# A recommender's user stage: some history rows fetched one by one from SyncE

## The chip, the core and the metric

The kernel runs on one core of a Trainium2 chip. A core has TensorE (PE), which multiplies matrices, VectorE (DVE) and ScalarE (ACT), which work on rows, GpSimd (POOL), which issues the gathers here, SyncE (SP), which issues plain transfers, and 16 DMA engines that carry out what is issued. The metric is device time in microseconds (us), lower is better. Each kernel is run several times; the number given is the median.

## What is computed

For 16384 users there are 100 history items each and one target item, out of 50001 items. Each item has an embedding of 64 values and two attention results of 32 values each over its 32 neighbours. The reference, cut to what matters:

```python
near_full = concat([near_pois, pad_row])
a_sus = _neighbor_attn(E_in, near_full)          # per item: softmax(E . E[near]) over 32 neighbours
a_inf = _neighbor_attn(E_out, near_full)
h = concat([E_hist[history], a_sus[history], a_inf[history]], -1)   # B x 100 x 128
t = concat([E_tgt[target], a_inf[target], a_sus[target]], -1)       # B x 128
x = h * t[:, None, :]
z = relu(einsum('bld,hd->blh', x, W1) + b1)
scores = einsum('blh,h->bl', z, W2[0])
exp_A = exp(scores) * ((history != target[:, None]) & (history != 0))
attn = exp_A / (sum(exp_A, -1) ** 0.5)[:, None]
s = sum(h * attn[..., None])                      # one number
pred = sigmoid(cosine(broadcast s, t))            # B
```

## The kernel before, in words

The work has two stages, and the second needs all of the first.

The item stage makes two tables in device memory. `table` holds one row of 128 floats (512 bytes) per item for use as history, `ttab` one per item for use as target. It goes through the items in 23 blocks; POOL gathers the neighbours' rows with one indirect transfer per neighbour (L111, `v`), VectorE and ScalarE do the attention, and SyncE writes the finished rows out (L163 `table`, L164 `ttab`). SyncE also loads each block's inputs (L102, L104, L106).

The user stage works on 128 users at a time, one to a partition. There are 128 such columns `c`. The 100 history places of a column are cut into 25 groups `g` of four. For a group, POOL issues four indirect transfers (L233): each fetches one history row for each of the 128 users into the tile `h`. PE turns the four blocks round (L246, `hT_ps`), VectorE multiplies them by the turned target row `tT` (L248, `xT`) and sums the plain rows (L249, `hsum`), PE applies W1 (L255, `z_ps`), ScalarE the relu (L257, `z`), and PE the vector W2, one column of `score` for each of the four places (L265). At the end of a column ScalarE and VectorE make the weights and two sums (L271 on).

The loop over `s` puts the groups of all columns in one row and works on three at once: `gather` and `turn` of group s, `hidden` of s-1, `scored` of s-2. Twelve `h` tiles let POOL run ahead by up to twelve groups. The target rows of the next column are gathered half way through a column (L197, `t`). The history numbers are loaded for four columns at a time, by SyncE (L193, `hidx`, 128 x 400 integers, two buffers); SyncE has nothing else to do in this stage until the result is written (L325). Each engine runs its own instructions in order; semaphores, which the framework sets, hold a reader until its writer is done. A transfer also waits for the one issued eight before it from the same kind of queue, since eight semaphores are used in turn.

Of the kernel before, what the change touches and what calls it, by code (L numbers as in the profile page):

```python
# [9 lines left out]

F32 = mybir.dt.float32
I32 = mybir.dt.int32
AF = mybir.ActivationFunctionType
ALU = mybir.AluOpType
AX = mybir.AxisListType

P = 128
ITEMS = 50001
# [3 lines left out]
D = 128  # L22
HID = 128
B = 16384
L = 100
# [10 lines left out]
UC = B // P  # L36
BSUB = 4
LG = 4
NG = L // LG


@with_exitstack
def kernel(
# [13 lines left out]
    nc = tc.nc  # L57
# [5 lines left out]
    table = dram.tile([ROWS, D], F32, name="table")  # L63
# [29 lines left out]
    with (  # L93
# [6 lines left out]
        for it in range(NITER):  # L100
            nidx = n_in.tile([P, NSUB, K], I32, name="nidx")
            nc.sync.dma_start(nidx, near_v[it])  # L102
# [5 lines left out]
            for j in range(NSUB):  # L108
                v = n_v.tile([P, K, 2, G], F32, name="v")
                for k in range(K):  # L110
                    nc.gpsimd.indirect_dma_start(  # L111
                        out=v[:, k].rearrange("p t d -> p (t d)"),
# [20 lines left out]
                for t in range(2):  # L133
                    nc.scalar.activation(  # L134
                        ex[:, t, :],
                        sc[:, t, :],
                        AF.Exp,
                        bias=top[:, t : t + 1],
# [32 lines left out]
    hist_v = history.rearrange("(p i j) l -> i p j l", p=P, j=BSUB)  # L171
    tidx = const.tile([P, UC], I32, name="tidx")
    nc.scalar.dma_start(tidx, target.rearrange("(p c) -> p c", p=P))
    tidf = const.tile([P, UC], F32, name="tidf")
    nc.vector.tensor_copy(tidf, tidx)
    with (
        tc.tile_pool(name="u_in", bufs=2) as u_in,
        tc.tile_pool(name="u_t", bufs=2) as u_t,
        tc.tile_pool(name="u_h", bufs=12) as u_h,
        tc.tile_pool(name="u_x", bufs=3) as u_x,  # L180
        tc.tile_pool(name="u_s", bufs=2) as u_s,
        tc.tile_pool(name="ps_t", bufs=3, space=bass.MemoryType.PSUM) as ps_t,
        tc.tile_pool(name="ps_z", bufs=3, space=bass.MemoryType.PSUM) as ps_z,
        tc.tile_pool(name="ps_s", bufs=2, space=bass.MemoryType.PSUM) as ps_s,
    ):
        users = {}
        hists = {}

        def target_rows(c):

            if c % BSUB == 0:
                hidx = u_in.tile([P, BSUB, L], I32, name="hidx")
                nc.sync.dma_start(hidx, hist_v[c // BSUB])  # L193
                hists[c // BSUB] = hidx

            t = u_t.tile([P, D], F32, name="t")
            nc.gpsimd.indirect_dma_start(  # L197
                out=t,
                out_offset=None,
                in_=ttab[0:ITEMS, :],  # L200
                in_offset=bass.IndirectOffsetOnAxis(ap=tidx[:, c : c + 1], axis=0),
            )
            users[c] = {"t": t, "hidx": hists[c // BSUB][:, c % BSUB, :]}

        def target_work(c):
            u = users[c]
            t = u["t"]
            tT_ps = ps_t.tile([P, LG, P], F32, name="hT_ps")
            nc.tensor.transpose(tT_ps[:, 0, :], t, ident)  # L209
            tT = u_t.tile([D, 1, P], F32, name="tT")  # L210
            nc.vector.tensor_copy(tT[:, 0, :], tT_ps[:, 0, :])  # L211
            u["tT"] = tT
            nc.vector.tensor_reduce(tsum[:, c : c + 1], t, AX.X, ALU.add)
            junk = u_t.tile([P, D], F32, name="junk")
            nc.scalar.activation(junk, t, AF.Square, accum_out=tsq[:, c : c + 1])
            idf = u_s.tile([P, L], F32, name="idf")
            nc.scalar.copy(idf, u["hidx"])  # L217
            keep = u_s.tile([P, L], F32, name="keep")
            nc.vector.tensor_scalar(keep, idf, 0.0, None, ALU.not_equal)
            nc.vector.scalar_tensor_tensor(  # L220
                keep, idf, tidf[:, c : c + 1], keep, ALU.not_equal, ALU.mult
            )
            u["keep"] = keep
            u["hsum"] = u_s.tile([P, L], F32, name="hsum")
            u["score"] = ps_s.tile([P, L], F32, name="score")
            u["xT"], u["z"] = {}, {}

        def gather(c, g):
            u = users[c]
            h = u_h.tile([P, LG, D], F32, name="h")  # L230
            for q in range(LG):
                l = g * LG + q
                nc.gpsimd.indirect_dma_start(  # L233
                    out=h[:, q, :],
                    out_offset=None,
                    in_=table,
                    in_offset=bass.IndirectOffsetOnAxis(ap=u["hidx"][:, l : l + 1], axis=0),
                )
            u["h", g] = h

        def turn(c, g):
            u = users[c]
            h = u.pop(("h", g))
            hT_ps = ps_t.tile([P, LG, P], F32, name="hT_ps")
            for q in range(LG):
                nc.tensor.transpose(hT_ps[:, q, :], h[:, q, :], ident)  # L246
            xT = u_x.tile([D, LG, P], F32, name="xT")
            nc.vector.tensor_tensor(xT, hT_ps, u["tT"].to_broadcast([D, LG, P]), ALU.mult)  # L248
            nc.vector.tensor_reduce(u["hsum"][:, g * LG : (g + 1) * LG], h, AX.X, ALU.add)  # L249
            u["xT"][g] = xT  # L250

        def hidden(c, g):
            u = users[c]
            z_ps = ps_z.tile([HID, LG, P], F32, name="z_ps")
            nc.tensor.matmul(z_ps, w1T, u["xT"].pop(g), start=True, stop=True)  # L255
            z = u_x.tile([HID, LG, P], F32, name="z")
            nc.scalar.activation(z, z_ps, AF.Relu, bias=b1_sb)  # L257
            u["z"][g] = z

        def scored(c, g):  # L260
            u = users[c]
            z = u["z"].pop(g)
            for q in range(LG):
                l = g * LG + q
                nc.tensor.matmul(  # L265
                    u["score"][:, l : l + 1], z[:, q, :], w2_sb, start=True, stop=True
                )
            if g < NG - 1:
                return
            ea = u_s.tile([P, L], F32, name="ea")  # L270
            nc.scalar.activation(ea, u["score"], AF.Exp)  # L271
            nc.vector.tensor_tensor(ea, ea, u["keep"], ALU.mult)
            nc.vector.tensor_reduce(den[:, c : c + 1], ea, AX.X, ALU.add)
            nc.vector.tensor_tensor(ea, ea, u["hsum"], ALU.mult)  # L274
            nc.vector.tensor_reduce(num[:, c : c + 1], ea, AX.X, ALU.add)
            del users[c]

        groups = [(c, g) for c in range(UC) for g in range(NG)]
        target_rows(0)
        for s in range(len(groups) + 2):  # L280
            if s < len(groups):
                c, g = groups[s]
                if g == 0:
                    target_work(c)
                if g == NG // 2 and c + 1 < UC:
                    target_rows(c + 1)
                gather(c, g)
                turn(c, g)
            if 1 <= s <= len(groups):
                hidden(*groups[s - 1])  # L290
            if s >= 2:
                scored(*groups[s - 2])


    with (
# [3 lines left out]
        root = f_s.tile([P, UC], F32, name="root")  # L299
        nc.scalar.activation(root, den, AF.Sqrt)  # L300
        part = f_s.tile([P, UC], F32, name="part")
# [6 lines left out]
        s = f_s.tile([P, 1], F32, name="s")  # L308
# [4 lines left out]
        nc.vector.tensor_scalar(n1, n1, float(D), EPS * EPS, ALU.mult, ALU.max)  # L313
        nc.scalar.activation(n1, n1, AF.Sqrt)
        n2 = f_s.tile([P, UC], F32, name="n2")
# [65 lines left out]
```

## Time and profile before

| what | value |
|---|---|
| time, median of 3 runs | 36303.63 us (36298.54 to 36312.89) |
| the profiled execution's own time | 31810.23 us |
| its span, first to last instruction | 31808.5 us |
| item stage, up to the last `ttab` write's issue | about 15642 us |
| user stage | about 16160 us |
| PE busy over the span | 15238.9 us (48%) |
| POOL busy over the span | 24005.7 us (75%) |
| VectorE / ScalarE busy | 8951.2 us (28%) / 2851.2 us (9%) |
| DMA from issue to landing, h / v / hidx | 2.5 / 2.4 / 2.5 us |

The profile is taken from one execution, which took less time than each of the three runs of the first row. Its durations belong to that execution. Busy time of an engine counts instructions that work on data; those that only issue, wait or set registers are not in it[...]. PE's busy time is modelled and can be too long. A line of the costliest groups reads: line, engine, operation, tile written from tiles read, shapes, count, then busy time and the mean of one in nanoseconds, then the idle time just before these instructions and what ended most of it. The slices show the whole span from left to right in 40 equal parts, each digit the busy share in tenths.

### The profile page before, as it was taken

The numbers are of one execution on the slowest core, as the hardware profiler recorded it, in microseconds if no ns is written. First come the engines' busy times: TensorE is split into PE (matmuls) and PEld (weight loads), VectorE is DVE, ScalarE is ACT, GpSimd is POOL, SyncE is SP. The second block draws the span as 40 slices with busy tenths as digits, with TensorE's granted clock in tenths as the row PEclk, the third lists the DMA queues.
The fourth block names the chain that finished last, engine by engine and source line by source line (L and its number), as shares of the span: only waits on it lengthen the run. The fifth ranks groups of instructions, "written<-read, shape, count | busy, mean of one in ns | idle before, by whom it ended". The sixth has DMA issues, their size and how long they took to land.

```text
span 31808.5 us, 154035 instructions
## 1 busy us (share of the span) xinstructions
PE 15238.9 (48%) x44931; PEld 9632.2 (30%) x44931; DVE 8951.2 (28%) x10957; ACT 2851.2 (9%) x6458; POOL 24005.7 (75%) x25446
## 2 busy tenths in 40 slices
PE   0000000000000000000299999999999999999999
PEld 0000000000000000000155555555555555555555
DVE  2222222222222222222222222222222222222222
ACT  0000000000000000000011111111111111111111
POOL 7777777777777777777777777777777777777777
PEclk9999999999999999999955555555555555555555
DMA  2111111111111111111122222222222222222221
GB/s 50 30 30 30 30 31 33 30 30 30 30 34 30 30 30 30 31 33 28 37 54 53 54 53 54 53 54 54 53 54 53 54 53 54 54 53 54 53 54 52
DMA packets 981064, 1358.75 MB, mean 43 GB/s; under 512 B 559872, under 2 KB 564352, under 8 KB 977280
## 3 DMA queue, kind: packets, MB, share of 16 engines
q0 software_dynamic: 814080, 1258.87, 17.1%
q1 hardware_dynamic: 115952, 77.16, 0.9%
q10 hardware_dynamic: 50192, 12.87, 0.2%
q8 instruction: 363, 5.95, 0.1%
q14 instruction: 477, 3.91, 0.0%
HBM read 1308.76 MB, written 51.30 MB: 43 GB/s over the span
## 4 chain that ended last, share of the span: by engine, by line
POOL 49%; issue 19%; PE 15%; DMA 14%; DVE 2%; ACT 1%; POOLq 0%; ACTq 0%; SPq 0%; DVEq 0%
POOL v L111 35%; POOL h L233 13%; DMA h<-table,hidx 11%; PE z_ps L255 7%; PE score L265 5%; PE hT_ps L246 3%; DMA v<-in_egeo_dram,nidx 2%; DVE xT L248 2%; ACT z L257 1%; POOL t L197 0%; POOLq L233 0%; DVE tT L211 0%; DVE ea L274 0%; DMA nidx<-in_near_dram 0%; DMA ttab<-trow 0%
## 5 line engine op out<-in xcount | busy, mean ns | idle before, releaser
L233 POOL DMA_INDIRECT h<-table,hidx x12800 | 12079.2, 944 | 3900.9 <-issue 3159.2
L111 POOL DMA_INDIRECT v<-in_egeo_dram,nidx x12512 | 11805.1, 943 | 3820.9 <-issue 3719.2
L209 PE MATMUL hT_ps<-ident,t 128*128 128x128 f32 x128 | 53.9, 421 | 15644.7 <-DMA t<-ttab,tidx 15644.7
L265 PEld LDWEIGHTS score<-w_sb,z 128*128 128x128 f32 x25600 | 6225.7, 334 | 1080.8 <-ACT z L257 1074.0
L255 PE MATMUL z_ps<-xT,w1T 128*128 128x512 f32 x6400 | 6526.7, 1123 | 0.0
L265 PE MATMUL score<-w_sb,z 128*128 128x1 f32 x25600 | 5903.9, 335 | 235.4 <-ACT z L257 150.2
L246 PE MATMUL hT_ps<-ident,h 128*128 128x128 f32 x12800 | 4715.0, 439 | 673.3 <-DMA h<-table,hidx 520.3
L249 DVE TENSOR_REDUCE hsum<-h 128x4 f32<-128x512 f32 x3200 | 2194.7, 686 | 9243.7 <-DMA h<-table,hidx 9226.9
L209 PEld LDWEIGHTS hT_ps<-ident,t 128*128 128x128 f32 x128 | 28.8, 225 | 15644.9 <-ACT idf L217 15644.9
L246 PEld LDWEIGHTS hT_ps<-ident,h 128*128 128x128 f32 x12800 | 2676.6, 209 | 5434.3 <-issue 3257.2
L120 DVE TENSOR_TENSOR prod<-v,own_ps 128x2048 f32<-128x2048 f32 x391 | 894.6, 2288 | 10794.7 <-DMA v<-in_egeo_dram,nidx 10794.4
L257 ACT ACTIVATE z<-z_ps,b_sb 128x512 f32<-128x512 f32 x3200 | 2199.1, 687 | 13448.3 <-PE z_ps L255 13335.1
L248 DVE TENSOR_TENSOR xT<-hT_ps,tT 128x512 f32<-128x512 f32 x3200 | 2210.2, 691 | 2028.6 <-PE hT_ps L246 2026.8
L255 PEld LDWEIGHTS z_ps<-xT,w1T 128*128 128x128 f32 x6400 | 1745.4, 332 | 0.0
L145 DVE TENSOR_TENSOR wv<-v,ex 128x1024 f32<-128x1024 f32 x782 | 1398.8, 1867 | 0.0
L118 ACT COPY own_ps<-own 128x64 f32<-128x64 f32 x391 | 84.4, 216 | 11499.9 <-DVE prod L120 11498.4
L127 DVE TENSOR_REDUCE sc<-prod 128x64 f32<-128x2048 f32 x391 | 894.5, 2288 | 13.4
L152 DVE TENSOR_REDUCE att<-wv 128x64 f32<-128x2048 f32 x391 | 893.8, 2286 | 13.4
L160 ACT COPY trow<-row 128x32 f32<-128x32 f32 x782 | 131.7, 215 | 2465.7 <-DVE row L153 2465.7
L134 ACT ACTIVATE ex<-sc,top 128x32 f32<-128x32 f32 x782 | 227.7, 291 | 1081.9 <-DVE top L130 1069.2
L142 DVE RECIPROCAL tot<-tot 128x2 f32<-128x2 f32 x391 | 64.8, 166 | 362.3 <-ACT ex L134 362.3
L197 POOL DMA_INDIRECT t<-ttab,tidx x128 | 120.7, 943 | 60.5 <-issue 60.5
(49 smaller groups left out, 808.6 us busy)
## 6 DMA issues: line engine op xcount, KB each, us to landing
h<-table,hidx POOLq DMA_INDIRECT x12800, 2.5
v<-in_egeo_dram,nidx POOLq DMA_INDIRECT x12512, 2.4
table<-row SPq DMA_DIRECT2D x23, 1088.0 KB, 4.4
own<-in_egeo_dram SPq DMA_DIRECT2D x23, 544.0 KB, 3.6
row<-in_ehist_dram SPq DMA_DIRECT2D x23, 544.0 KB, 6.7
ttab<-trow SPq DMA_DIRECT2D x23, 544.0 KB, 6.8
ttab<-in_etgt_dram ACTq DMA_DIRECT2D x1, 12500.0 KB, 53.5
hidx<-in_history_dram SPq DMA_DIRECT2D x32, 200.0 KB, 2.5
```

What stands on the lines that cost most here:

```text
L111: nc.gpsimd.indirect_dma_start(out=v[:, k].rearrange("p t d -> p (t d)"), out_offset=None, in_=egeo, in_offset=bass.IndirectOffsetOnAxis(a ...
L120: nc.vector.tensor_tensor(prod.rearrange("p k t d -> p k (t d)"), v.rearrange("p k t d -> p k (t d)"), own_ps.to_broadcast([P, K, 2 * G]), ...
L127: nc.vector.tensor_reduce(sc.rearrange("p t k -> p k t"), prod, AX.X, ALU.add)
L145: nc.vector.tensor_tensor(wv[:, t].rearrange("p d k -> p k d"), v[:, :, t, :], ex[:, t, :].rearrange("p (k o) -> p k o", o=1).to_broadcast ...
L152: nc.vector.tensor_reduce(att, wv, AX.X, ALU.add)
L233: nc.gpsimd.indirect_dma_start(out=h[:, q, :], out_offset=None, in_=table, in_offset=bass.IndirectOffsetOnAxis(ap=u["hidx"][:, l : l + 1], ...
L246: nc.tensor.transpose(hT_ps[:, q, :], h[:, q, :], ident)
L248: nc.vector.tensor_tensor(xT, hT_ps, u["tT"].to_broadcast([D, LG, P]), ALU.mult)
L249: nc.vector.tensor_reduce(u["hsum"][:, g * LG : (g + 1) * LG], h, AX.X, ALU.add)
L255: nc.tensor.matmul(z_ps, w1T, u["xT"].pop(g), start=True, stop=True)
L257: nc.scalar.activation(z, z_ps, AF.Relu, bias=b1_sb)
L265: nc.tensor.matmul(u["score"][:, l : l + 1], z[:, q, :], w2_sb, start=True, stop=True)
```

## The change

The four-group runs of each column that start at g = 0, 4, 8, 12, 16 and 20 are counted through all columns, and every 42nd of them is taken out of POOL's hands: 18 runs in all. For such a run, SyncE goes through the 128 partitions one after the other. For each, it loads 16 byte offsets from the tile `hoff` into registers with one instruction, and issues 16 transfers of one row (512 bytes) each into the tile `hs`, each at the offset in a register. There are two `hs` tiles. The first run is asked for ahead of the loop, each following one where the loop reaches the run before it. `gather` of such a group issues nothing and hands out a part of `hs`.

The byte offsets are the item numbers times 512, by a shift on VectorE into `hoff`. The load of the history numbers goes from SyncE to POOL, and four blocks ahead of use in place of one; `hidx` and `hoff` have six buffers each.

```diff
+UG = 4
+UNIT = 42
+AHEAD = 4
...
-        tc.tile_pool(name="u_in", bufs=2) as u_in,
+        tc.tile_pool(name="u_in", bufs=AHEAD + 2) as u_in,
...
+        tc.tile_pool(name="u_hs", bufs=2) as u_hs,
...
+        table_b = table.bitcast(U8).rearrange("(o r) d -> o (r d)", o=1)
+
+        def history_of(i):
+            hidx = u_in.tile([P, BSUB, L], I32, name="hidx")
+            nc.gpsimd.dma_start(hidx, hist_v[i])
+
+            hoff = u_in.tile([P, BSUB, L], I32, name="hoff")
+            nc.vector.tensor_scalar(hoff, hidx, 9, None, ALU.logical_shift_left)
+            hists[i] = hidx, hoff
+
         def target_rows(c):
 
-            if c % BSUB == 0:
-                hidx = u_in.tile([P, BSUB, L], I32, name="hidx")
-                nc.sync.dma_start(hidx, hist_v[c // BSUB])
-                hists[c // BSUB] = hidx
...
+        early = {}
+
+        def one_by_one(c, g):
+
+            hs = u_hs.tile([P, UG * LG, D], F32, name="hs")
+            hoff = hists[c // BSUB][1]
+            for p in range(P):
+                _, vals = nc.values_load_multi_w_load_instructions(
+                    hoff[p : p + 1, c % BSUB, g * LG : (g + UG) * LG],
+                    engines=[E.SP],
+                    min_val=0,
+                    max_val=(ITEMS - 1) * 4 * D,
+                    skip_runtime_bounds_check_because="worked out from an item's number",
+                )
+                for q in range(UG * LG):
+                    nc.sync.dma_start(
+                        hs[p : p + 1, q, :].bitcast(U8), table_b[:, ds(vals[q], 4 * D)]
+                    )
+            for i in range(UG):
+                early[c, g + i] = hs[:, i * LG : (i + 1) * LG, :]
+
         def gather(c, g):
             u = users[c]
+            if (c, g) in early:
+                u["h", g] = early.pop((c, g))
+                return
...
         groups = [(c, g) for c in range(UC) for g in range(NG)]
+        units = [(c, g) for c in range(UC) for g in range(0, NG - UG + 1, UG)]
+        units = units[UNIT - 1 :: UNIT]
+        for i in range(AHEAD):
+            history_of(i)
+        one_by_one(*units[0])
         target_rows(0)
         for s in range(len(groups) + 2):
+            if s % (BSUB * NG) == 0 and AHEAD + s // (BSUB * NG) < UC // BSUB:
+                history_of(AHEAD + s // (BSUB * NG))
+            if s < len(groups) and groups[s] in units[:-1]:
+                one_by_one(*units[units.index(groups[s]) + 1])
```

More of the change, by code (lines that the diff above doesn't have):

```diff
@@ L12 @@
 I32 = mybir.dt.int32
+U8 = mybir.dt.uint8
+E = mybir.EngineType
 AF = mybir.ActivationFunctionType
@@ L202, in target_rows @@
             )
-            users[c] = {"t": t, "hidx": hists[c // BSUB][:, c % BSUB, :]}
+            users[c] = {"t": t, "hidx": hists[c // BSUB][0][:, c % BSUB, :]}
         def target_work(c):
```

## The prediction

> **What bounds the kernel now.** I read the page first: the slices, then the chain of waits, then the costliest groups. After that I read the timeline of a few microseconds of the user stage, the busy times of the whole stage, and the SyncE queue.
>
> ```profile
> PE   0000000000000000000299999999999999999999
> POOL 7777777777777777777777777777777777777777
> PEclk9999999999999999999955555555555555555555
> ...
> POOL 49%; issue 19%; PE 15%; DMA 14%; DVE 2%; ACT 1%; POOLq 0%; ACTq 0%; SPq 0%; DVEq 0%
> ...
> L233 POOL DMA_INDIRECT h<-table,hidx x12800 | 12079.2, 944 | 3900.9 <-issue 3159.2
> ...
> L246 PE MATMUL hT_ps<-ident,h 128*128 128x128 f32 x12800 | 4715.0, 439 | 673.3 <-DMA h<-table,hidx 520.3
> ```
>
> The span has two halves. In both, POOL is busy 7 tenths without a break. PE works only in the second half, 9 tenths busy at half clock. Two engines could pace that half, so the page alone does not decide. The timeline does (start, duration, engine, operation, idle time before):
>
> ```profile
> 20002.54 0.94 POOL L233 DMA_INDIRECT h<-table,hidx  x1 [0.30 <-issue]
> 20003.79 0.94 POOL L233 DMA_INDIRECT h<-table,hidx  x1 [0.30 <-issue]
> 20005.04 0.94 POOL L233 DMA_INDIRECT h<-table,hidx  x1 [0.30 <-issue]
> 20006.28 0.94 POOL L233 DMA_INDIRECT h<-table,hidx  x1 [0.30 <-issue]
> ```
>
> One gather starts every 1.248 us: 0.944 busy plus 0.304 that is always there and waits for nothing. The busy times of the user stage, asked as one window, confirm it:
>
> ```profile
> core 0: us, PE busy (x) PEld busy (x) DVE busy (x) ACT busy (x) POOL busy (x), PEclk, DMA share, GB/s
> 15672.00:31784.00 16112.00, 15212.26 (x44858) 9616.28 (x44857) 4576.22 (x7403) 2298.48 (x3698) 12178.98 (x12907) 0.51 0.21 53
> ```
>
> 16112 / 12907 = 1.2483 us per POOL transfer, so POOL never waits for a buffer. A group of four history rows takes 16112 / 3200 = 5.03 us, and PE's own work in it is at most 15212 / 3200 = 4.75 us. POOL is the bound; PE has 0.28 us per group (5.6%) in hand.
>
> SyncE is nearly idle, but it is the engine that gets the work. Its issues back to back at the start and at a late place (the second line in each pair follows at once), its load of history numbers, and the packets of the two hardware queues:
>
> ```profile
> 56.44 0.43 SPq L104 DMA_DIRECT2D own<-in_egeo_dram  x1
> 56.92 0.57 SPq L106 DMA_DIRECT2D row<-in_ehist_dram  x1
> ...
> 702.37 0.33 SPq L163 DMA_DIRECT2D table<-row  x1
> 702.75 0.59 SPq L164 DMA_DIRECT2D ttab<-trow  x1
> ...
> L193 SPq DMA_DIRECT2D hidx<-in_history_dram x32: 327/328/426, 15648.2 to 30782.8; - x32
> ...
> q1 hardware_dynamic: 115952, 77.16, 0.9%
> q10 hardware_dynamic: 50192, 12.87, 0.2%
> ```
>
> An issue on SyncE costs 0.33 us at least, plus 0.05 us until the next (702.37 + 0.33 = 702.70, next at 702.75).
>
> **What the Trainium skill says.** "DMA: Bandwidth & Descriptors", section "Why a DMA increments its semaphore by 16 and not by 1": a transfer is cut over up to 16 engines by its slowest dimension that is not 1, and each engine used posts its share of the semaphore. The trace agrees: the ACT queue moved 50000 rows of 256 B, 128 rows of tidx and one single row of 64 floats; 50000 + 128 + 16 + 3 x 16 = 50192, the count shown, only if the single row went as 16 pieces. So a 512 B row will be 16 pieces of 32 B and 16 semaphore packets. The register loads are in no row of the trace. The same page, "Latency and other measured facts", puts a floor of about 0.6 us under one such load; "Runtime: NRT & Kernel Launch", "Instruction fetch mechanics", gives about 0.2 us per register, thus an estimate of 3.2 us for 16. No run here shows either yet.
>
> **The change part by part.**
>
> *Gathers removed.* There are 128 x 6 = 768 runs of four groups, every 42nd is taken: 18 runs, 18 x 16 = 288 gathers. 288 x 1.248 = 359 us off POOL, on the path. Their work on PE, DVE and ACT stays.
>
> *History numbers moved to POOL.* 32 plain transfers of 128 descriptors, as many as one gather has. No plain POOL transfer is in the trace: 0.3 us each (the issue gap alone) to 2 us; I take a gather's 1.25. Four stand ahead of the first target row, where POOL sat idle for 21.8 us (15627.2 to 15649.1) until the last ttab rows had landed, and are hidden. 28 x 1.25 = 35 us stay (8 to 56). POOL queues only gathers behind them, and their buffers (six now) were released two blocks earlier, so there is no wait. The 32 issues that SyncE loses were on no path.
>
> *Shift on DVE.* 32 x 128x400. The nearest row is L219's 128x100 at 0.204 us, so about 0.45 to 0.8 each, 14 to 26 us in all. DVE is busy 28% of the stage; it hides there, and at worst costs the 26. Behind a shift that waits for its transfer (2.5 us to land) xT of the same group queues, which waits for later gathers anyway.
>
> *SyncE's fetch.* Per run 128 register loads m and 2048 single-row issues r. r: 0.33 + 0.05 = 0.376 us; bounds 0.37 and 0.42 (the 0.09 us gap at 15641 instead of 0.05). Each row waits for the row eight before it; rows land in some 1.5 to 2.5 us (out_dram 1.5, hidx 2.5), 8 x 0.376 = 3.0, so that wait should rarely show. m: 0.6 to 3.2 us. T = 2048 r + 128 m: 758 + 77 = 835 us at the lowest, 860 + 410 = 1270 at the highest. I take r = 0.376 and m between the floor and the Runtime page's 1.3 us for a load of several registers: 770 + 77 to 166 = 847 to 936.
>
> *The room for it.* Two runs in use lie 175 groups apart: 684 gathers + 7 target rows + 1.75 history transfers = 693 POOL transfers, 693 x 1.248 = 865 us. There are two hs buffers, so SyncE fetches one run ahead and no more. PE's 175 x 4.75 = 831 us fit as well. While PE works on a run of hs, POOL gathers up to 12 groups ahead; nothing is lost there.
>
> *DMA engines.* 36864 rows x 32 packets = 1.18 million. The queues above show 0.009 x 16 x 31808 / 115952 = 0.040 us and 0.002 x 16 x 31808 / 50192 = 0.020 us per packet, so 24 to 47 ms over 16 engines, 9 to 18% of the stage on top of the 21% shown. Not full; a gather may land later, but landing is not what paces POOL.
>
> *Sum, if T fits.* 359 - 35 = 324 us off the profiled execution of 31810.23 (span 31808.5 and 1.7 around it): 31486.
>
> **How that stands to the median.** The runs shown take 36303.63, 4493 us more than the profiled execution, and no view says where. Only POOL works all along; spread over its 25440 gathers it is 0.177 us each, so 1.425 instead of 1.248. If PE made it, a group would take 5.03 + 4493 / 3200 = 6.43 us, and PE's clock would have to lie near 0.37, below any value granted here. I take POOL as the likelier. Then the saving is 260 x 1.425 = 370 us, and the room per run 693 x 1.425 = 987. If the 4493 us lie outside the stage, it is 324 and 865. Between them I forecast 36303.6 - 353 = 35950; its own range is 35880 to 36060.
>
> **The rivals.**
>
> *SyncE becomes the bound (slower).* Place: PE waits for hs at the first transpose of each run, POOL fills its 12 buffers and stops. Price: 18 x (T - room) less the saving. It decides from T = 865 + 18 = 883 at the trace's POOL rate, or 987 + 21 = 1008 at the slower one. For it: my T spans both points, and 0.2 us per register would settle it: 770 + 410 = 1180, 18 x 193 - 370 = +3100, 39400. With m = 1.9, half way, and r = 0.42 it is 1103: 18 x 116 - 370 = +1720. Against: the 0.2 us is stated for loads from HBM, here they come from SBUF. Its likely time is about 37700, half way between break-even and 39400 rounded.
>
> *Nothing changes.* The small packets slow each gather: 0.03 us on 12500 gathers takes back 375 us; or PE is the real limit in the runs shown and gathers were hidden. Then 36250 to 36350, I say 36290. Against: landing does not enter POOL's 0.304 us, and PE's clock.
>
> *The change does less than it says.* If the scheduler put the row transfers late, runs would wait; but the order of SyncE's queue holds nothing else in the stage, and each batch starts with its buffer. No separate chance.
>
> **How the numbers follow.** Fits: 0.60. SyncE bound: 0.32. Nothing: 0.08. Likeliest time 35950. The range starts at 35880 (0.03 below). SyncE's cases reach from break-even to 41000; cutting at 37800 leaves out some 0.15 of the whole. A difference within 0.2% (73 us) is what measurement cannot tell from none. Faster 0.60, same 0.08, slower 0.32.
>
> **What would show it.** Right: POOL's transfers at 1.25 us throughout, idle time on SyncE between a run's last row and the release of its buffer, hs transposes without waits. Wrong: SyncE issuing rows from end to end, PE waiting for DMA hs<-table for tens of us per run with POOL idle beside it; a register load above 1.5 us or a row above 0.42 would be the cause. A busy time per gather above 0.944 would speak for the packets.

## The result, and the profile after

| | median us | against the kernel before |
|---|---|---|
| before | 36301.08 (36296.01 to 36312.89, 4 runs) | |
| changed | 41162.86 (41105.69 to 41164.45, 4 runs) | 1.1335 (95% interval 1.1315 to 1.1355) |

The changed kernel is 13.3% slower. Its profiled execution (span 41103.9 us) is of the timed kind (it takes as long as the timed runs), unlike the 31810 us execution of the kernel before that was shown. From the changed kernel's page, the slices and the costliest groups:

```profile
PE   0000000000000000065556655566555665557555
...
POOL 7777777777777777764445544455444554446544
PEclk9999999999999999965555555555555555555555
...
L270 POOL DMA_INDIRECT h<-table,hidx x12512 | 11825.6, 945 | 11509.1 <-PE hT_ps L222 4917.0
L117 POOL DMA_INDIRECT v<-in_egeo_dram,nidx x12512 | 13389.0, 1070 | 4106.4 <-issue 3996.6
...
L283 PE MATMUL hT_ps<-ident,hs 128*128 128x128 f32 x288 | 87.5, 411 | 4674.8 <-DMA hs<-table 4674.6
```

In the user stage POOL is now busy 4 to 6 tenths and PE 5 or 6 with one 7, against 7 and 9 in the 31810 us execution (6 and 7 in a timed execution of the kernel before, shown below). The last line says who stands in the way: 288 transposes of hs, four groups of four for each of 18 runs, have 4675 us of idle time before them, practically all of it for the row transfers. The waits of PE and the timeline of SyncE show the same from both sides (engine, tile and line, what it waited for: us, times, longest; then start, duration, engine, transfers in one stretch):

```profile
PE hT_ps L283 <- DMA hs<-table: 4674.6, 18, 274.0
```

```profile
24028.07 1022.35 SPq L256 DMA_DIRECT2D hs<-table  x1416
...
25059.74 240.39 SPq L256 DMA_DIRECT2D hs<-table  x580
```

Eighteen waits, one for each run, of 260 us on average. SyncE issues without a stop from the first row at 17535 us to the last at 40804: 18 runs in 23269 us, T = 1293 us each. Its waits for a row eight before add up to only 396 us of that. The 55 groups from the last run on fill the remaining 300 us. The second fence tells more: it is nearly all of one run, the first stretch with the other engines at work and the second while PE and POOL stood waiting. A row cost 1022.35 / 1416 = 0.722 us in the first and 240.39 / 580 = 0.414 us in the second, its share of the register loads included.

### The profile page after: what moved, and what is told of

Its sections match the earlier page's. It is cut to its first block, busy times and chain, and to the rows that moved or that the text cites. A ratio compares the mean times of both kernels' runs of the same rounds, so it can differ in the third digit from the quotient of the medians.

```text
span 41103.9 us, 229500 instructions
## 1 busy us (share of the span) xinstructions
PE 13883.8 (34%) x44931; PEld 9305.7 (23%) x44931; DVE 8668.9 (21%) x10989; ACT 2845.6 (7%) x6458; POOL 25355.1 (62%) x25190
## 3 DMA queue, kind: packets, MB, share of 16 engines
q1 hardware_dynamic: 185072, 89.63, 0.8%
## 5 line engine op out<-in xcount | busy, mean ns | idle before, releaser
L270 POOL DMA_INDIRECT h<-table,hidx x12512 | 11825.6, 945 | 11509.1 <-PE hT_ps L222 4917.0
L117 POOL DMA_INDIRECT v<-in_egeo_dram,nidx x12512 | 13389.0, 1070 | 4106.4 <-issue 3996.6
L302 PEld LDWEIGHTS score<-w_sb,z 128*128 128x128 f32 x25600 | 5805.3, 320 | 5330.0 <-ACT z L294 3964.7
L302 PE MATMUL score<-w_sb,z 128*128 128x1 f32 x25600 | 5641.8, 329 | 3720.2 <-ACT z L294 3342.6
L292 PE MATMUL z_ps<-xT,w1T 128*128 128x512 f32 x6400 | 6286.8, 1084 | 1283.6 <-issue 1093.2
L283 PE MATMUL hT_ps<-ident,h 128*128 128x128 f32 x12512 | 3818.2, 416 | 6.2 <-DMA h<-table,hidx 5.3
L283 PEld LDWEIGHTS hT_ps<-ident,h 128*128 128x128 f32 x12512 | 3061.6, 255 | 2805.4 <-issue 2763.4
L286 DVE TENSOR_REDUCE hsum<-h 128x4 f32<-128x512 f32 x3128 | 2098.4, 676 | 23.7 <-DMA h<-table,hidx 15.9
L283 PE MATMUL hT_ps<-ident,hs 128*128 128x128 f32 x288 | 87.5, 411 | 4674.8 <-DMA hs<-table 4674.6
```

The lines of the kernel that those rows point to most:

```text
L117: nc.gpsimd.indirect_dma_start(out=v[:, k].rearrange("p t d -> p (t d)"), out_offset=None, in_=egeo, in_offset=bass.IndirectOffsetOnAxis(a ...
L270: nc.gpsimd.indirect_dma_start(out=h[:, q, :], out_offset=None, in_=table, in_offset=bass.IndirectOffsetOnAxis(ap=u["hidx"][:, l : l + 1], ...
L302: nc.tensor.matmul(u["score"][:, l : l + 1], z[:, q, :], w2_sb, start=True, stop=True)
```

## The experiments

Theory A at the start: SyncE needs longer for a run than the room (the time between two runs in use), because its instructions are slower than priced. Rival B: the changed kernel slows all engines by its traffic, whether the rows come in time or not. Each kernel with a single execution is beside one or more of the kernel before on the same chip; those gave 36251 to 36355 us, so that 0.3% there is no difference.

**The kernel before, traced again.**

> The kernel before, unchanged, for a trace of an execution that takes the 36300 us of the timed runs (the profiled execution shown took 31810). Theory A (SyncE's fetch of a run takes longer than the room for it, and SyncE sets the end): this run shows the item stage at about 17500 us as in the changed kernel's trace, gathers of 1.40 us there, and a user stage of about 18800 us with POOL as the pace. Theory B (the changed kernel slows every other engine by its traffic, also in the item stage): gathers here take 1.25 us in both stages and the span is near 31800.

36352.08 us. Its page, slices and groups:

```profile
PE   0000000000000000000477777777777777777777
...
POOL 7777777777777777777666666666666666666666
PEclk9999999999999999999855555555555555555555
...
L233 POOL DMA_INDIRECT h<-table,hidx x12800 | 12083.4, 944 | 6517.4 <-issue 3588.8
L111 POOL DMA_INDIRECT v<-in_egeo_dram,nidx x12512 | 13306.0, 1063 | 4192.3 <-issue 4090.4
L265 PE MATMUL score<-w_sb,z 128*128 128x1 f32 x25600 | 5898.5, 335 | 4125.0 <-ACT z L257 3300.0
```

The item stage takes 17517 us, as in the changed kernel's trace: the neighbours' gathers start every 1.40 us instead of 1.25. So B is out for that stage. The user stage takes 18.8 ms, 5.88 us a group, but not with POOL as the pace, as the expectation under A had it: history gathers still take 944 ns and 0.30 us to the next, and POOL is idle for 6517 - 3589 = 2900 us more than that. It is ahead and waits for buffers: 99 of 100 history gathers start ten groups or more ahead of VectorE's sum over the same rows (there are twelve tiles), in the 31810 us execution about one group ahead. PE is the one that lacks input. The timeline shows how:

```profile
25012.42 2.05 PE L255 MATMUL z_ps<-xT,w1T 128*128 128x512 f32 x2
25012.57 0.94 POOL L233 DMA_INDIRECT h<-table,hidx  x1 [0.30 <-issue]
...
25014.27 0.85 PE L246 MATMUL hT_ps<-ident,h 128*128 128x128 f32 x3
...
25015.06 0.94 POOL L233 DMA_INDIRECT h<-table,hidx  x1 [0.30 <-issue]
25018.53 0.69 ACT L257 ACTIVATE z<-z_ps,b_sb 128x512 f32<-128x512 f32 x1 [7.99 <-remote]
25018.54 0.69 DVE L248 TENSOR_TENSOR xT<-hT_ps,tT 128x512 f32<-128x512 f32 x1 [7.04 <-remote]
25018.77 0.94 POOL L233 DMA_INDIRECT h<-table,hidx  x1 [2.77 <-remote]
...
25019.27 0.59 PE L265 MATMUL score<-w_sb,z 128*128 128x1 f32 x2 [4.15 <-ACT z L257]
```

The z_ps that ScalarE needs was done by 25014.5, yet ScalarE starts at 25018.5, together with VectorE and shortly before POOL; "remote" stands for a releaser that the trace does not hold. PE then starts after 4.15 us of idle time. Idle stretches of more than 2 us between two matmuls, called pauses here, come 731 times in the stage, 3154 us in all; otherwise groups mostly follow each other every 4.73 us, PE's own pace at half clock. In the 31810 us execution there is not one.

SyncE differs as well. One of its instructions in the item stage, whose semaphore changes in neither trace at that time, took (shortest, median, longest, in ns; first the 31810 us execution, then this one):

```profile
L163 SPq EVENT_SEMAPHORE  x23: 17/17/17, 690.6 to 14963.2; - x23
...
L163 SPq EVENT_SEMAPHORE  x23: 17/710/710, 742.0 to 16753.0; - x23
```

In 21 of 23 blocks SyncE is held for 0.70 or 0.71 us there, although the kernel is the same and no row is fetched. Every later trace has the same, in 18 to 22 of the 23.

**The history numbers on POOL alone.** No run is taken out of POOL's hands.

```diff
-        units = units[UNIT - 1 :: UNIT]
+        units = []
...
-        one_by_one(*units[0])
```

> Only the part of the change that loads the history numbers on POOL and shifts them on VectorE; SyncE fetches no row and all 12800 gathers stay. Theory A: no loss, 36300 to 36380 us (28 transfers more on POOL at 1.3 us). Theory B, in the form that the new history load disturbs: above 37000.

36347.0 us beside 36354.92: that part costs nothing. One such load takes POOL 0.55 us in the changed kernel's trace and the 0.30 after it.

**Every 64th run, and every 84th.**

```diff
-UNIT = 42
+UNIT = 64
```

> Every 64th run instead of every 42nd: 12 runs, 267 groups apart. SyncE needs 1290 us for a run in the changed kernel's trace; the room for 267 groups is 267 x 5.9 = 1570 us at the rate of the 36300 us runs. Theory A: the loss is gone, 35950 to 36250 us, and SyncE waits at the end of each run. Theory B (each fetched row costs the other engines time, wherever it lies): the loss shrinks only with the number of rows, 36300 + 4860 x 12 / 18 = 39500.

> Every 84th run: 9 runs, 350 groups apart, room 350 x 5.88 = 2058 us against 1490 us for a run at its slowest so far. SyncE has a quarter of the time free. Theory S: no gain, 36350 to 36500 us, as the gathers that go were not the pace and the rows still cost the others a little (205 us for 12 runs, so about 150 for 9). Theory P: about 36150 us.

36560.11 us beside 36354.92 for 12 runs. For 9 runs, 36413.85 beside 36260.85, ratio 1.0042 (1.0026 to 1.0059). The big loss is gone as soon as a run fits, so SyncE's lateness is what cost 4860 us. But there is no gain either; for 9 runs there is a small loss outside the noise. The stretch of one run in the timeline of every 64th:

```profile
20527.13 1491.95 SPq L256 DMA_DIRECT2D hs<-table  x2044
```

With PE and POOL never held up, a run takes 1492 us, longer than the 1293 of the changed kernel, where SyncE had quiet times while it was waited for.

**Fixed offsets.** The register loads and moves are left out, and the rows fetched are others.

```diff
-                _, vals = nc.values_load_multi_w_load_instructions(
-                    hoff[p : p + 1, c % BSUB, g * LG : (g + UG) * LG],
...
-                        hs[p : p + 1, q, :].bitcast(U8), table_b[:, ds(vals[q], 4 * D)]
+                        hs[p : p + 1, q, :].bitcast(U8), table_b[:, ds((p * UG * LG + q) * 4 * D, 4 * D)]
```

> The offsets of the row transfers are constants, so the 2304 register loads and the 36864 register moves are left out; the rows fetched are not the history's. Theory A with the register work as the cause: 128 x 1.24 us of loads and 2048 x 0.09 us of moves go from 1290 us, about 950 us for a run, which fits: about 35950 to 36300 us. Theory A with the transfers' own issue as the cause: still above 1100 us for a run, about 38500 us or more.

36456.2 us beside 36354.92. A run takes 840 us and fits:

```profile
29992.96 839.85 SPq L249 DMA_DIRECT2D hs<-table  x2047
```

With 18 runs as in the changed kernel, 288 gathers gone and SyncE in time, the kernel is still no faster. So the forecast saving fails on its own, apart from SyncE's lateness.

**The gathers left out.** For the chosen runs nothing is fetched, and what follows is computed of zeros.

```diff
+        hs = u_hs.tile([P, UG * LG, D], F32, name="hs")
+        nc.vector.memset(hs, 0.0)
...
-            for p in range(P):
-                _, vals = nc.values_load_multi_w_load_instructions(
...
-                for q in range(UG * LG):
-                    nc.sync.dma_start(
...
```

> The 18 runs' rows are left out: POOL does not gather them, SyncE does not fetch them, and what is computed of them is of zeros. This is the most that the change could bring. Theory P (POOL sets the pace of the user stage, as in the profiled execution that the prediction was read from): 288 gathers at 1.43 us go, about 35950 us. Theory S (in the timed executions PE's own 4.73 us per group and the pauses of all engines set the pace, and POOL waits for buffers): 36270 to 36360 us, no gain that counts.

> Every second run is left out in the same way: 6144 of 12800 gathers, nothing in their place. Theory G (the pauses come from the traffic of the gathers): the user stage falls from 18830 us to 15150 (3200 groups at 4.73) if the pauses go, or to about 17000 if half of them stay: 32700 to 34600 us. Theory N (the pauses have another source, such as the instructions of PE, VectorE and ScalarE): 36250 to 36350 us, as before.

With 18 runs left out 35980.74 us beside 36260.85, ratio 0.9923 (0.9907 to 0.9940): 280 us, between the two theories, or 0.97 us a gather. This is the most that there was to win. POOL's pace is an unlikely source, as POOL was ahead. In the trace PE goes to full clock at each left-out run; in most of them several groups in it or just after it follow each other every 2.1 us instead of 4.7, and PE stands at full clock for 1328 us of the stage instead of 461. With every second run left out, 31631.3 us, and the page shows a higher clock:

```profile
PEclk9999999999999999999999766666666666666666
```

620 pauses are left in a stage of 14.1 ms, and they take 3143 us, as much as with all gathers. PE stands at full clock for 4065 us of that stage. The time fell below the 32700 us that the end of all pauses would have given, through the clock, which neither theory had.

**The rows beside all gathers.** As with every 64th run, but `hs` is not read and all 12800 gathers stay.

```diff
-            for i in range(UG):
-                early[c, g + i] = hs[:, i * LG : (i + 1) * LG, :]
```

> SyncE fetches the 12 runs of every 64th into hs, but nothing reads them and POOL gathers all 12800 as before. Against the kernel with every 64th run (36560) this separates the two halves of the change. Theory S: near 36560, since the gathers' going brought nothing; the 205 us over the kernel before are the price of the row traffic for the other engines. Theory P: the gathers' going brought some 270 us there, so this one takes about 36830.

38441.99 us, above both, but not for a reason that either named. In the stage SyncE stopped twice, for 2127 and 2629 us, for offsets that VectorE shifted late; so its last two runs were left for the end, and PE stood idle for 1829 us while SyncE issued them:

```profile
SPq L248 <- DVE hoff L203: 2629.0, 1, 2629.0
```

Up to there it took about 36600 us, as Theory S had it. Those last rows are worth more than the total. Three stretches of one run each, the first beside the other engines, the others with all of them done:

```profile
20479.98 1452.94 SPq L256 DMA_DIRECT2D hs<-table  x2048
...
36737.08 846.85 SPq L256 DMA_DIRECT2D hs<-table  x2042
...
37587.96 846.19 SPq L256 DMA_DIRECT2D hs<-table  x2040
```

849 us for a full run when undisturbed, 1453 beside the others: the same 2048 rows and 128 loads. It is not the transfers alone that take longer. Before each, a register move (MOVE) is run, which issues nothing; its shortest, median and longest durations in ns, in the changed kernel and then in the undisturbed run here:

```profile
L256 SPq MOVE hs<-table x36864: 1/29/1472, 17534.7 to 40804.4; - x200
...
L256 SPq MOVE hs<-table x2043: 29/29/29, 36737.0 to 37584.0; - x186
```

In the changed kernel the moves add up to 4060 us, where 29 ns each would be 1069. So SyncE's stream of instructions is held, and rows that land late are not the reason (396 us of waits for them in 23269).

**Who disturbs SyncE.** Rows from fixed places that nothing reads, once in the item stage, where POOL gathers and PE is idle, and once in a user stage in which 96 of 100 gathers are left out and what follows is computed of zeros. The edit of the first:

```diff
+            if 4 <= it < 12:
+                sc = n_sc.tile([P, 4, D], F32, name="rows")
+                for p in range(P):
+                    for q in range(4):
+                        o = (p * 4 + q) * 4 * D
+                        nc.sync.dma_start(
+                            sc[p : p + 1, q, :].bitcast(U8), egeo_b[:, o : o + 4 * D]
+                        )
```

> The kernel before, and in 8 of the 23 blocks of the item stage SyncE also issues 512 transfers of 512 B each from fixed places into a tile that nothing reads. There POOL gathers without a break, VectorE works a quarter of the time and PE not at all. With fixed offsets a row took 0.295 us when undisturbed and 0.41 us on average in the user stage. Theory G (the gathers' traffic slows SyncE's instructions): 0.38 us a row or more here. Theory I (the instructions of PE, VectorE and ScalarE slow it): 0.30 to 0.32 us here.

> The opposite: in the user stage all runs of four groups are left out (4 of 100 gathers stay, the rest is computed of zeros), so PE, VectorE and ScalarE work on with hardly a gather, and SyncE issues 16384 rows from fixed places that nothing reads. Theory G: 0.30 to 0.32 us a row while PE works. Theory I: 0.41 us or more.

The first took 36279.89 us beside 36281.07. From the SyncE timeline, the first kernel's and then the second's:

```profile
3070.46 619.55 SPq L116 DMA_DIRECT2D rows<-in_egeo_dram  x443
```

```profile
17999.82 4000.14 SPq L315 DMA_DIRECT2D sc<-table  x13432
```

Beside gathers without a break a row takes 619.55 / 443 = 1.40 us, which is the gathers' own step there. Nearly without gathers, with PE busy 9 tenths, it takes 4000.14 / 13432 = 0.298 us. Theory G holds here, and more strongly than it was put. Both kernels ran in executions of the timed kind; no run put a queue of rows beside gathers in one like the 31810 us execution. The second kernel shows two further things. It took 24919.64 us, thus 7.4 ms for the user stage, 2.3 us a group; and its clock was 9 tenths or more in every slice (0.96 on average in the stage), with 5 pauses in place of 731:

```profile
PE   0000000000000000000000000000799999999999
...
PEclk9999999999999999999999999999999999999999
```

So in such executions the pauses of the other engines need the gathers, though they do not go with their number; the gathers alone do not bring them, since the 31810 us execution had all gathers and no pause. PE's half clock goes with the gathers, not with the pauses: it was there in that execution too.

**A deeper order of the groups.** An attempt at a faster kernel: PE's work placed further behind the turning.

```diff
-            if 1 <= s <= len(groups):
-                hidden(*groups[s - 1])
-            if s >= 2:
-                scored(*groups[s - 2])
+            if 2 <= s <= len(groups) + 1:
+                hidden(*groups[s - 2])
+            if s >= 4:
+                scored(*groups[s - 4])
```

> The kernel before with hidden two groups and scored four groups behind turn (one and two before), and six buffers for xT and z; no row fetched by SyncE. PE waited 3300 us for ScalarE's z in the trace of 36350 us. Theory D (in a pause PE only lacks input, because VectorE and ScalarE stand still): the wait is covered in part, 34500 to 35700 us. Theory E (a pause stops PE itself as well): 36200 to 36350 us.

36275.6 us beside 36281.07, ratio 0.9999 (0.999 to 1.0008): no difference, as Theory E had it. No kernel that computes everything was faster than the kernel before.

## Why the prediction failed, by its steps

*Which engine sets the pace.* Read rightly from an execution that is not the one timed. The gap of 4493 us to the median was put down to POOL in both stages, 1.425 us a gather. The item stage bears that out (1.40 us, 1870 us of the gap). In the user stage it is wrong: gathers stay at 1.25 us, and PE at half clock together with the pauses makes 5.88 us a group. Hence 353 us of saving was forecast where at most 280 were to be had, with PE at full clock for longer and not with a faster POOL. The argument that PE's clock would have to lie near 0.37 for this left pauses out of account.

*SyncE's fetch.* This is the step that decided: the term r was mis-sized. It was put at 0.376 us a row and measured 0.56 us in the changed kernel (with the register move, from one row's first instruction to the next), and 0.66 us with every 64th run, where nobody waits. The 0.376 us came from single issues, and from the 31810 us execution, in which SyncE was not held where all timed ones hold it (17 ns against 710 above). Which of the two made the price wrong was not separated.

The sum T = 847 to 936 us holds for a quiet core (849 measured), but in part by luck: there a row took 0.333 us, 0.063 of it for the register move, which had no term, and a load 1.31 us to the next instruction. Even the 0.05 us between two issues was one place; at 22 of 23 such places the trace before had 0.09 to 0.11. Beside gathers T was 1293 us in the changed kernel and 1414 to 1521 us where nobody waits. The change in r is the whole of it; the register load m, on which the range of T hung, takes 1.24 us (median of 2304), inside the bounds that were taken from the floor and the Runtime page's 1.3 us (both as the prediction cites them), and far from the 0.2 us a register of the same page, which is stated for loads from HBM.

The Trainium skill's "DMA: Bandwidth & Descriptors", section "Issuing engines are not separate DMA queues", says that starting transfers from several engines at once saves only the issuer's time, which is usually small beside the transfer itself. Here that time was the cost: 0.30 us without gathers, 1.40 us beside them.

*The room.* 987 us was forecast; 175 x 5.877 = 1028 us were there. 18 x (1293 - 1028) = 4770 us, against 4754 us between the two traces. The rival "SyncE becomes the bound" thus named the place, the wait and POOL's stop after 12 groups as they came, with chance 0.32; its price was set by the loads and came out at 1400 us over before instead of 4860 (half way to 39400, as it was meant, would have been 1550).

*The DMA engines.* A row was said to go as 16 pieces. The hardware queue of SyncE shows

```profile
q1 hardware_dynamic: 185072, 89.63, 0.8%
```

115952 - 32 x 144 for the history load that moved + 36864 x 2 = 185072: one piece and one semaphore packet a row. The rule that the prediction takes from the page stands, but the row was read wrongly. In the trace the single row between two tables in device memory is recorded as 16 elements of 16 B, a row of hs as one element of 512 B; so a cut by the dimension that the instruction carries gives 16 for the one and 1 for the other. Nothing depended on it, as the engines were far from full either way.

*The rival that nothing changes.* It comes near to what remains where a run fits: fetching costs about what it saves, or more. From every 84th run: 153 us of loss and 140 us of saving forgone (half of 280) over 18432 rows, 0.016 us a row that the others lose; by this estimate 2048 rows cost 33 us and replace 16 gathers worth 15.5 us. Every 64th gives 0.016 too, fixed offsets 0.010, both from single executions.

*What stays open.* What the pauses are, and why the execution shown first had none, 1.25 us gathers in the item stage and a SyncE that was not held, was not settled; all later executions had the pauses, 1.40 us and the hold. That the gathers have a part in most of the pauses is shown by their near absence without gathers; by what path they hold up SyncE and the others is not.

## What to carry to other kernels

Price an instruction that is to run beside another engine's stream from a place where the two run together and in numbers, in an execution that takes the timed runs' time, not from single issues between long waits; a queue of them can take its step from the other stream. Before a profile is used to say what sets the pace, compare its execution's time with the timed runs, and if they differ by far more than the expected gain, treat the pace as unknown. And a plan that replaces one POOL instruction by 128 transfers must pay for all 128 out of what that one instruction cost, also for what the transfers take from the rest: here 0.016 us each was already too much.

## What was not expected of the hardware

- A 512 B transfer issued from SyncE took 0.294 us with a fixed offset and 0.323 us with one in a register when undisturbed (medians, from one to the next), and 1.40 us beside indirect transfers that POOL issues without a break; the gathers were not slowed by it (1.395 us while the rows went, 1.400 after).
- SyncE's register moves were held too, for up to 1.47 us in place of 0.029.
- Loading 16 registers from on-chip memory took SyncE 1.24 us.
- PE ran at half clock for nearly all of a user stage with gathers, and at full clock for 6711 of 7378 us in the one nearly without, although it was busier there: 4.73 and 2.3 us a group. The Trainium skill's "TensorE: Matmul & The Clock Gate", section "What's actually happening", ties the clock to how busy PE was in a window of about 3.4 us. The trace agrees in one point: with all gathers the stretches at full clock last 3.4, 6.8 or 10.2 us. The pauses do not explain the half clock, as the 31810 us execution had it for 15796 of 16151 us without a pause; what does was not tried.
